# A four-layer graph network on one core: the drain of the attention layer re-ordered, the weight products taken in seven quarters, some normalising moved to GpSimd

## The chip, the core and the metric

The kernel runs on one core of a Trainium2 chip. The metric is the device time of one execution in microseconds (us); lower is better. Three runs of the kernel before took 2685.5 to 2687.25, with a median of 2686.97 us.

## The reference

Four graph layers work on x (4096 rows of 256) and one dense adjacency matrix adj (4096 x 4096), all in float32. Each layer is added to its input and normalised:

```python
x = _layernorm(x + L0(x, adj, adj, Wqkv, bqkv, Wout, bout, graph_bias))
x = _layernorm(x + L1(x, adj, W, a))
x = _layernorm(x + L2(x, adj, W, b))
x = _layernorm(x + L3(x, adj, W))
```

L0 is attention with 4 heads of 64: the scores are `qh @ kh.T / 8 + graph_bias * adj`, masked where adj is 0, then softmax, the product with v, and Wout. L1 is a graph attention: `softmax(leaky_relu(e_src[:, None] + e_dst[None, :]))` under the mask, times `x @ W`. L2 is `adj_norm @ x @ W.T + b` and L3 is `relu(adj_norm @ x @ W)`, where adj_norm is adj scaled by the inverse roots of its row sums on both sides.

## The kernel before

It is written so that the order of the instructions on each engine follows from a loop over steps (`manual_schedule`); every engine works through its own list in order and waits by semaphores.

**Layer 0 (lines 217 to 770).** A unit is 128 rows and one pair of heads; there are 64 units of four steps, and a step covers 1024 of the 4096 columns. `step(t)` (L543) runs units in a pipeline: `score` (TensorE products into two PSUM tiles `sc[0]` and `sc[1]`, L411, then VectorE adds the bias and takes the maximum, L422), four steps later `expo` (ScalarE, L438), then `turn` (sixteen transposes of 64 x 128 blocks on TensorE into one PSUM tile `ptr`, L452, and a copy to SBUF as `pt`, L460 on ScalarE or L458 on VectorE), one step later `attend` (TensorE, 32 records into `po`, L470). The row sums of a unit go from VectorE (L482 to L491) through a DMA to memory (`norm`, L493) and a second DMA that spreads them (`rb`, L514), both from GpSimd's queue; `scale` (L521) multiplies `po` with them two steps after they are sent, `finish` (L376, `pp`) applies Wout. When no unit is left to score, the last unit is drained: these are the steps nd to nd+7 (nd is 256).

Beside the last two units and the drain, the list `tail` runs the start of layer 1: the finished rows are read back in eight parts of 512 rows (`load_part`, SP's queue), the inverse deviations of all but two row blocks come from a Newton iteration (`ln_newton`, L135 to L146, its sixteen later operations on GpSimd), `norm_part` (L149, four operations of 128 x 256 on VectorE) normalises a part and writes it out from GpSimd's queue, and `turn_half` (L663) transposes a part's two column halves with four 128 x 128 transposes each into `sc[0]` or `sc[1]`, from which ScalarE (L667) or VectorE (L669) copies them. The part buffers belong to a pool of seven, which the bias tiles of layer 0 and the masks of layer 1 share. `project_ed` (L682, `ped`) and `project_w` (L163) are the first products of layer 1; the list of step nd+7 begins them.

**Layer 1 (lines 840 to 1050).** A unit is 128 rows with 4 steps. `gat_step(t)` issues for step t, in this order: `score` of t (VectorE, mask L877 and L879), `attend` of t-10 (TensorE, L938), `turn` of t-6 (VectorE, L928), `expo` of t-5 (ScalarE, L921), and `leaky` of t-2 (ScalarE, L892). The maxima of a unit are combined in its fourth to fifth step (L899 to L918), in front of the turns. `attend` of a unit needs all four of its turned blocks. The products `project_w` of the other parts fill TensorE meanwhile; DMAs of their results (`e_src`, `es_q`) run beside them.

**Layers 2 and 3 (lines 1050 to the end).** The product with adj is done by blocks of 1024 output rows (two halves of 512): 16 steps to a block, 4 blocks to a layer, and in each step 7 products of 128 x 128 by 128 x 512 (L1113) in place of 8 (a Strassen scheme), each in a PSUM bank of its own (`m0` to `m6`). VectorE forms the sums of adj blocks that they need one step ahead (`sums`, L1077 to L1080); for layer 3 a row pair is prepared at the end of a step (`prepare`, L149, L819, L822 to L826). After a block's last step `keep` copies the seven results out, `combine` forms the transposed hidden rows `hT` on VectorE in the next two steps, and `rows(n)` then multiplies 128 of them with W2 or W3: two products of 128 x 256 into the one PSUM bank that is left (`py`, L1144), and VectorE adds the result onto the row (L1161; in layer 3 after a ReLU on ScalarE, L1166 and L1167) and takes its statistics. There are eight `rows` to a block, two in each of four steps: one after the third product of the step ("mid") and one behind its last ("end"). The very last block has a routine of its own (`end`), which is not changed.

A matrix product in float32 stands in the trace as two records with a weight load each; a transpose stands as one.

Of the kernel before, what the change touches and what calls it, by code (L numbers as in the profile page):

```python
# [8 lines left out]
F32 = mybir.dt.float32  # L9
# [38 lines left out]
def tile_gnn(  # L48
# [70 lines left out]
    def ln_stats(pool, row, ci):  # L119
        st = pool.tile([P, 6], F32, tag="bnst", name="bnst")  # L120
        nc.vector.bn_stats(st, row)
        nc.vector.bn_aggr(mv[:, ci, :], st)
# [24 lines left out]

    def ln_apply(dst, src, ci):
        nc.vector.tensor_scalar(  # L149
            dst, src, mv[:, ci, 0:1], rstd[:, ci : ci + 1], ALU.subtract, ALU.mult  # L150
        )
# [43 lines left out]
    with ExitStack() as l0:  # L195
# [195 lines left out]
        class Pair:  # L391
# [53 lines left out]

            def turn(self, k, j, by_dve=False):
                pa = ps_t.tile([P, 2, CS, HD], F32, tag="tr", name="ptr")
                z = self.z[j][k]
                for c in range(CS):
                    for r in range(2):  # L450
                        half = slice(r * HD, (r + 1) * HD)
                        nc.tensor.transpose(  # L452
                            pa[:, r, c, :], z[half, c * P : (c + 1) * P], ident[half, half]
                        )
                pt = pp_.tile([P, CS, P], F32, tag="pt", name="pt")
                to = pt.rearrange("p c (r i) -> p r c i", r=2)
                if by_dve:
                    nc.vector.tensor_copy(to, pa)  # L458
                else:
                    nc.scalar.copy(to, pa)  # L460
                self.pt[j][k] = pt
# [69 lines left out]
        def step(t):  # L531
# [29 lines left out]
            if turns:  # L561
                pairs[ut].turn(kt, 0)
            if expos:
                pairs[ue].expo(ke, 1)
# [28 lines left out]
            elif edges:  # L593
                edges.pop().make_edges()
            if turns:
                pairs[ut].turn(kt, 1, by_dve=not live)
            if attends and ka == NS - 2:
# [47 lines left out]

        def norm_part(j, a0, a1):
            xs = parts[j]
            for a in range(a0, a1):
                ci = a * NJ + j
                ln_apply(xs[:, a, :], rows[ci].xr if ci == NCH - 1 else xs[:, a, :], ci)  # L650
            if a1 == NA:
                nc.gpsimd.dma_start(
                    x0.rearrange("(a j p) e -> p a j e", p=P, j=NJ)[:, :, j, :], xs
                )

        def turn_half(j, cc, by_act):

            if cc == 0:
                turned_x[j] = zp.tile([P, 2, NSB, NA, QB], F32, tag="z", name="xt1")
            xs = parts.pop(j) if cc else parts[j]  # L660
            px = sc[cc][:, 0:512].rearrange("p (a i) -> p a i", i=P)
            for a in range(NA):
                nc.tensor.transpose(px[:, a, :], xs[:, a, cc * P : (cc + 1) * P], ident)  # L663
            to = turned_x[j][:, cc, :, :, :]
            px = px.rearrange("p a (b r) -> p b a r", r=QB)
            if by_act:
                nc.scalar.copy(to, px)  # L667
            else:
                nc.vector.tensor_copy(to, px)  # L669

        def turn_part(j, split=False):
            for cc in range(2):
                turn_half(j, cc, split and cc == 0)

# [20 lines left out]
        def last_rstd():  # L695
# [10 lines left out]
        edp = []  # L706
        n0, nd = n_steps - 2 * NS, n_steps
        tail = {
            n0: [(load_weights,), (load_part, 0)],
            n0 + 1: [(load_part, 1), (weight, 0, 1)],  # L710
            n0 + 2: [(load_part, 2), (weight, 1, 1), (ln_newton, 0, NCH - 2)],
            n0 + 3: [(norm_part, 0, 0, NA)],
            n0 + 4: [(load_part, 3), (norm_part, 1, 0, NA)],
            n0 + 5: [(load_part, 4), (norm_part, 2, 0, NA)],
            n0 + 6: [(load_part, 5), (weight, 0, 0), (weight, 1, 0)],
            n0 + 7: [(norm_part, 3, 0, NA), (turn_part, 0, True)],
            nd: [(load_part, 6), (turn_part, 1), (norm_part, 4, 0, NA), (load_part, 7)],
            nd + 1: [(turn_part, 2), (norm_part, 5, 0, NA)],
            nd + 2: [(turn_part, 3), (norm_part, 6, 0, NA - 1)],
            nd + 3: [(turn_part, 4), (norm_part, 7, 0, NA - 1)],  # L720
            nd + 4: [(turn_half, 5, 0, True)],
            nd + 6: [(turn_half, 5, 1, False)],
            nd + 7: [
# [3 lines left out]
                (norm_part, 7, NA - 1, NA),  # L727
                (turn_part, 6, True),
                (turn_part, 7, True),
                (project_w, 0, 0, sc[0]),  # L730
# [116 lines left out]
    with ExitStack() as l1:  # L847
# [110 lines left out]
        def at(t):  # L958
            u, s = divmod(t, NSB)
            return (units[u], s) if 0 <= t < n_t else (None, s)  # L960

        def gat_step(t):
# [5 lines left out]
            if folds:  # L968
                folds.gather_max()
            u, s = at(t)  # L970
            if u:
# [4 lines left out]
            if u:  # L976
                u.attend(s)
            u, s = at(t - NSB - 2)
            if u:
                u.turn(s)  # L980
            u, s = at(t - NSB - 1)
# [72 lines left out]
    with ExitStack() as l2:  # L1054
# [29 lines left out]
        order = (2, 3, 0, 1, 4, 5, 6)  # L1084

        class Block:
            def __init__(self, layer, jb):
# [63 lines left out]

            def rows(self, n):

                h, s = divmod(n, NSJ)
                ci = h * NP + self.jb * NSJ + s
                py = ps_m.tile([P, 512], F32, tag="y", name="py")
                for f in range(2):
                    self.weigh(n, py, f)
                row = xc[:, ci, :]
                if self.layer == 0:  # L1160
                    nc.vector.scalar_tensor_tensor(  # L1161
                        row, py[:, 0:D], d2[:, ci : ci + 1], row, ALU.mult, ALU.add
                    )
                else:
                    r = wk.tile([P, D], F32, tag="relu", name="relu")
                    nc.scalar.activation(r, py[:, 0:D], AF.Relu, scale=d3[:, ci : ci + 1])  # L1166
                    nc.vector.tensor_tensor(row, row, r, ALU.add)  # L1167
                ln_stats(wk, row, ci)

# [122 lines left out]
        def at_step(t, when, f, *args):  # L1292
            later.setdefault((t, when), []).append((f, args))
# [6 lines left out]
        with tc.manual_schedule():  # L1300
            sums(0)
            ln_rstd(NCH - 1, NCH)
            blk = None
            for t in range(n_all):
# [20 lines left out]
                if c == NP - 1:  # L1325
# [3 lines left out]

                    r0 = t + 2 + 2 * (tl == T1 - 1)  # L1330
                    for n in range(2 * NSJ):
                        at_step(r0 + n // 2, ("mid", "end")[n % 2], blk.rows, n)
                    at_step(r0 + NSJ, "mid", block_rstd, jb)
# [6 lines left out]
                    if layer == 1:  # L1340
                        for h in range(2):
                            at_step(t + 3 + NSJ + h, "end", blk.store, h)

# [50 lines left out]
```

## Time and profile before

| | us |
|---|---|
| median of three runs | 2686.97 |
| the profiled execution | 2685.98 |
| its span from the first to the last instruction | 2684.2 |
| TensorE busy in it | 2669.1 |
| VectorE busy | 2187.9 |
| ScalarE busy | 1639.5 |
| GpSimd busy | 399.2 |

In the span layer 0 lasts until about 1366 us, its drain begins at about 1339, layer 1's row products run from 1404.9 to 1849.9 and layers 2 and 3 from 1850.1 on. A line of a timeline gives the start in us, the time it lasts, the engine (PE is TensorE, PEld its weight loads, DVE VectorE, ACT ScalarE, POOL GpSimd), the line of the kernel, the tiles written and read, the shape and the number of instructions merged in it; in brackets is the time for which the engine stood before it and what ended that. A matmul's end is modelled, so the pace of products is read from their starts.

### The profile page before, as it was taken

The page shows a single profiled execution, that of the slowest core. Times are in us where ns is not written, and L with a number is a line of the kernel's source. Part 1 is how long each engine was busy: PE and PEld are TensorE (multiplying, and loading weights), DVE is VectorE, ACT ScalarE, POOL GpSimd, SP SyncE. Part 2 cuts the span into 40 slices and gives each one's busy share as a digit, 9 for nine tenths or more (in the row PEclk, how much of TensorE's full clock was granted, in tenths as well). Part 3 has the DMA queues.
Part 4 walks back from the last instruction along what each step waited for, and adds up shares of the span by engine and source line. Part 5 has one row for each costly group of instructions (what it writes and reads, how often), then busy time and mean ns, then how long its engine had stood idle before and what let it go on. Part 6 is the DMA issues. An engine that isn't in the chain of part 4 may idle for free.

```text
span 2684.2 us, 59105 instructions
## 1 busy us (share of the span) xinstructions
PE 2669.1 (99%) x23834; PEld 1832.7 (68%) x23834; DVE 2187.9 (82%) x4120; ACT 1639.5 (61%) x2678; POOL 399.2 (15%) x701
## 2 busy tenths in 40 slices
PE   9999999999999999999999999999999999999998
PEld 6777777777777777777778888886444444444444
DVE  5999999999999999999879988886966578676565
ACT  2999999999999999999867766672100001000001
POOL 1222232232222222222220000001200000000000
PEclk9999999999999999999999999999999999999999
DMA  7444444444444444444372222222544545455543
GB/s 165 90 93 94 93 92 95 93 91 96 92 90 98 91 93 97 89 94 97 107 222 80 78 72 79 73 78 76 177 157 162 171 157 173 157 165 180 173 162 112
DMA packets 680339, 312.38 MB, mean 116 GB/s; under 512 B 554144, under 2 KB 584736, under 8 KB 680064
## 3 DMA queue, kind: packets, MB, share of 16 engines
q1 hardware_dynamic: 655968, 264.97, 39.3%
q0 software_dynamic: 22144, 42.05, 4.3%
q8 instruction: 186, 3.05, 0.5%
q10 hardware_dynamic: 1952, 1.58, 0.2%
q14 instruction: 89, 0.73, 0.1%
HBM read 262.40 MB, written 46.09 MB: 115 GB/s over the span
## 4 chain that ended last, share of the span: by engine, by line
PE 97%; DVE 1%; DMA 1%; issue 0%; POOL 0%; ACT 0%; DVEq 0%; POOLq 0%; ACTq 0%
PE m L1113 29%; PE po L470 18%; PE sc L411 17%; PE po L938 17%; PE ptr L452 11%; PE py L1144 2%; PE pv L266 1%; PE pk L245 1%; PE pp L376 1%; PE pq L354 1%; PE sc L163 0%; DVE pt L458 0%; DMA e_src<-esd 0%; DMA norm<-lt 0%; DVE z L422 0%
## 5 line engine op out<-in xcount | busy, mean ns | idle before, releaser
L422 DVE CUSTOM_DVE_ANT_0 z<-sc,bias 128x1024 f32<-128x1024 f32 x512 | 606.2, 1222 | 44.7 <-PE sc L411 44.6
L438 ACT ACTIVATE z<-z,nm 128x1024 f32<-128x1024 f32 x512 | 591.5, 1155 | 0.0
L460 ACT COPY pt<-ptr 128x1024 f32<-128x1024 f32 x507 | 511.0, 1008 | 66.6 <-PE ptr L452 66.0
L411 PE MATMUL sc<-store,qT 64*128 64x512 f32 x2048 | 504.1, 604 | 0.7 <-DVE mx L422 0.5
L470 PE MATMUL po<-pt,xc 128*64 128x128 f32 x8192 | 504.1, 276 | 0.1
L470 PEld LDWEIGHTS po<-pt,xc 128*64 128x64 f32 x8192 | 442.1, 137 | 17.7 <-DVE pt L458 0.3
L938 PE MATMUL po<-store,pt 128*128 128x257 f32 x2048 | 445.4, 379 | 1.5 <-issue 1.5
L452 PEld LDWEIGHTS ptr<-ident,z 64*128 64x128 f32 x8192 | 323.1, 138 | 177.6 <-issue 87.8
L938 PEld LDWEIGHTS po<-store,pt 128*128 128x128 f32 x2048 | 387.3, 189 | 59.5 <-issue 1.8
L452 PE MATMUL ptr<-ident,z 64*128 64x64 f32 x8192 | 357.4, 225 | 1.6 <-DVE pt L458 1.3
L1113 PE MATMUL m<-asum,ysum 128*128 128x512 f32 x672 | 324.7, 592 | 0.0
L411 PEld LDWEIGHTS sc<-store,qT 64*128 64x128 f32 x2048 | 194.4, 188 | 117.0 <-issue 108.8
L1113 PEld LDWEIGHTS m<-asum,ysum 128*128 128x128 f32 x672 | 127.7, 190 | 160.3 <-issue 139.7
L335 POOL DMA_DIRECT2D edge<-mk x256 | 143.7, 561 | 554.8 <-ACT mk L329 538.9
L1077 DVE TENSOR_TENSOR asum<-a,a 128x512 f32<-128x512 f32 x128 | 88.1, 688 | 150.8 <-PE m L1113 150.8
L1113 PE MATMUL m<-asum,store 128*128 128x512 f32 x448 | 210.5, 592 | 0.0
L1113 PE MATMUL m<-a,ysum 128*128 128x512 f32 x448 | 210.5, 592 | 0.0
L318 DVE SCALAR_TENSOR_TENSOR bias<-rt,gb,u 128x512 f32<-128x512 f32 x256 | 194.2, 759 | 9.1
L928 DVE STREAM_TRANSPOSE pt<-z 128x1024 f32<-128x1024 f32 x128 | 158.1, 1237 | 40.4 <-PE po L938 39.5
L1119 ACT COPY e<-m 128x512 f32<-128x512 f32 x28 | 16.2, 586 | 277.3 <-PE m L1113 277.3
L312 DVE STREAM_TRANSPOSE rt<-raw 128x512 f32<-128x512 f32 x256 | 180.0, 703 | 6.8 <-DMA raw<-in_adjT 6.5
L329 ACT ACTIVATE mk<-rt 128x512 bf16<-128x512 f32 x256 | 158.7, 620 | 10.0 <-DMA edge<-mk 5.9
(167 smaller groups left out, 2666.4 us busy)
## 6 DMA issues: line engine op xcount, KB each, us to landing
a<-in_adjT SPq DMA_DIRECT2D x256, 512.0 KB, 4.8
raw<-in_adjT SPq DMA_DIRECT2D x512, 128.0 KB, 3.9
edge<-mk POOLq DMA_DIRECT2D x256, 128.0 KB, 2.4
mk<-edge SPq DMA_DIRECT2D x256, 128.0 KB, 2.9
xq<-in_xT SPq DMA_DIRECT2D x32, 128.0 KB, 3.8
xr<-in_x SPq DMA_DIRECT2D x32, 128.0 KB, 3.0
x<-xs POOLq DMA_DIRECT2D x8, 512.0 KB, 6.0
xc<-x SPq DMA_DIRECT2D x8, 512.0 KB, 6.2
```

The source lines that it names most:

```text
L312: nc.vector.transpose(rt.rearrange("p (b r) -> p b r", r=QB), self.raw_now[:, half * nb : (half + 1) * nb, :],)
L318: nc.vector.scalar_tensor_tensor(self.bias[k][:, m0 : m0 + HT], rt, gb, u, ALU.mult, ALU.add)
L329: nc.scalar.activation(mk, rt, AF.Copy, accum_out=self.rs[:, j : j + 1])
L411: nc.tensor.matmul(ps[j][:, q * 512 : (q + 1) * 512], self.rows.qT[j * HD : (j + 1) * HD, self.pr, :], kT[j * HD : (j + 1) * HD, self.pr, ...
L422: nc.vector.tensor_tensor_reduce(z, sc[j], self.rows.bias[k], 1.0, NEG, ALU.add, ALU.max, self.mx[:, j, k : k + 1],)
L438: nc.scalar.activation(z, z, AF.Exp, bias=self.nm[:, j : j + 1], accum_out=self.ls[:, j, k : k + 1],)
L452: nc.tensor.transpose(pa[:, r, c, :], z[half, c * P : (c + 1) * P], ident[half, half])
L460: nc.scalar.copy(to, pa)
L470: nc.tensor.matmul(self.po[j * HD : (j + 1) * HD, 0:P], v_sb[:, ci, h * HD : (h + 1) * HD], self.pt[j][k][:, c, :], start=(ci == 0), stop= ...
L928: nc.vector.transpose(self.pt[:, :, s, :], self.z[s].rearrange("p (b r) -> p b r", r=QB))
L938: nc.tensor.matmul(self.po[:, 0 : D + 1], self.pt[:, b, :, :].rearrange("p s i -> p (s i)"), wh[:, b, :], start=(b == 0), stop=(b == NBK - 1),
L1113: nc.tensor.matmul(self.m[i], left, right, start=(c == 0), stop=(c == NP - 1))
```

## The change

There are four parts.

1. *Normalising.* `ln_newton` is issued two steps earlier (n0 in place of n0+2, where n0 is 248, the first step of the last unit but one to be scored). `norm_part` for parts 0 to 2 and three quarters of parts 6 and 7 goes to GpSimd; parts 3 to 5 stay on VectorE, one step later each.
2. *Drain.* With no scores left, the second `turn` of a step is done into `sc[1]` and directly behind the first, and before `attend`. The parts are turned into `sc[0]` alone, one half before `attend` and one behind it, by sixteen transposes of 64 rows in place of eight of 128; part j is turned in step nd+j (before: parts 0 to 4 in the steps nd-1 to nd+3, part 5 in nd+4 and nd+6). Part 7 is turned into two other PSUM tiles.
3. *Layer 1's start.* In its first ten steps `turn` is issued in front of `score` on VectorE.
4. *Weights.* The product of the hidden rows with W2 or W3 is done for both row halves at once with seven products of 128 x 128 by 128 x 128 in place of four of 128 x 128 by 128 x 256 (the Strassen scheme again). Sums of the weights are formed once and sums of `hT` once a block, on GpSimd. `weigh_shared` (four products, "mid") is copied out by ScalarE and summed up by four GpSimd operations; one step later `rows` (three products, "end") is added to that by VectorE, and both row blocks follow. The rows come two to three steps later than before, and with them the row rates, the preparation for layer 3 of the last block, and the stores.

In the program as it is built the weight sums stand in GpSimd's list in front of the first preparation of layer 2. VectorE's first operation on a layer-1 mask stands in the fourth step of the drain, between the copies of the two halves of part 3.

```diff
     def turn(self, k, j, in_scores=False):
+                if in_scores:
+                    pa = sc[1].rearrange("p (r c i) -> p r c i", r=2, i=HD)
+                else:
+                    pa = ps_t.tile([P, 2, CS, HD], F32, tag="tr", name="ptr")
...
             if turns:
                 pairs[ut].turn(kt, 0)
+            if turns and not live:
+                pairs[ut].turn(kt, 1, in_scores=True)
+            for f, *args in inner.get(t, ()):
+                f(*args)
             if expos:
                 pairs[ue].expo(ke, 1)
...
-            if turns:
-                pairs[ut].turn(kt, 1, by_dve=not live)
+            if turns and live:
+                pairs[ut].turn(kt, 1)
...
             for a in range(NA):
-                nc.tensor.transpose(px[:, a, :], xs[:, a, cc * P : (cc + 1) * P], ident)
+                for r in range(2):
+                    half = slice(r * HD, (r + 1) * HD)
+                    nc.tensor.transpose(
+                        px[:, r, a * HD : (a + 1) * HD],
+                        xs[half, a, cc * P : (cc + 1) * P],
+                        ident[half, half],
+                    )
...
+        inner = {nd + i: [(turn_half, i, 0, sc[0])] for i in range(6)}
         tail = {
-            n0: [(load_weights,), (load_part, 0)],
+            n0: [(load_weights,), (load_part, 0), (ln_newton, 0, NCH - 2)],
...
-            n0 + 2: [(load_part, 2), (weight, 1, 1), (ln_newton, 0, NCH - 2)],
-            n0 + 3: [(norm_part, 0, 0, NA)],
-            n0 + 4: [(load_part, 3), (norm_part, 1, 0, NA)],
-            n0 + 5: [(load_part, 4), (norm_part, 2, 0, NA)],
+            n0 + 2: [(load_part, 2), (weight, 1, 1)],
+            n0 + 3: [(norm_part, 0, 0, NA, gp)],
+            n0 + 4: [(load_part, 3), (norm_part, 1, 0, NA, gp)],
+            n0 + 5: [(load_part, 4), (norm_part, 2, 0, NA, gp)],
...
-            n0 + 7: [(norm_part, 3, 0, NA), (turn_part, 0, True)],
-            nd: [(load_part, 6), (turn_part, 1), (norm_part, 4, 0, NA), (load_part, 7)],
+            nd: [(turn_half, 0, 1, sc[0]), (load_part, 6), (norm_part, 3, 0, NA), (load_part, 7)],
+            nd + 1: [(turn_half, 1, 1, sc[0]), (norm_part, 4, 0, NA)],
...
-                (turn_part, 6, True),
-                (turn_part, 7, True),
+                (turn_half, 6, 0, sc[0], True),
+                (turn_half, 6, 1, sc[1]),
+                (turn_last, 7),
...
+            turns = at(t - NSB - 2)
+            soon = t < NSB + 6
+            if soon and turns[0]:
+                turns[0].turn(turns[1])
             u, s = at(t)
             if u:
                 u.score(s)
...
+            def hidden_sums(self):
+                self.hs = self.e[:, 0:4, :]
+                tt, hs, hT = nc.gpsimd.tensor_tensor, self.hs, self.hT
+                tt(hs[:, 0, :], hT[:, 1, 0, :], hT[:, 1, 1, :], ALU.add)
...
+            def weigh_shared(self, s):
+                py = ps_m.tile([P, 512], F32, tag="y", name="py")
...
+                self.small(py, 0, self.hT[:, 0, 0, rs], w[:, 0, 0:P])
+                self.small(py, 1, self.hs[:, 0, rs], ws[:, 0, :])
+                self.small(py, 2, self.hs[:, 2, rs], ws[:, 2, :])
+                self.small(py, 3, self.hs[:, 1, rs], ws[:, 1, :])
...
+                nc.scalar.copy(e[:, 0:4, :].rearrange("p i e -> p (i e)"), py)
+                tt = nc.gpsimd.tensor_tensor
+                tt(e[:, 4, :], e[:, 0, :], e[:, 3, :], ALU.add)
+                tt(e[:, 3, :], e[:, 1, :], e[:, 2, :], ALU.add)
+                tt(e[:, 3, :], e[:, 3, :], e[:, 4, :], ALU.add)
+                tt(
+                    e[:, 1:3, :],
+                    e[:, 1:3, :],
+                    e[:, 4, :].unsqueeze(1).to_broadcast([P, 2, P]),
+                    ALU.add,
+                )
...
-                for f in range(2):
-                    self.weigh(n, py, f)
...
+                self.small(py, 0, self.hT[:, 0, 1, rs], w[:, 1, 0:P])
+                self.small(py, 1, self.hs[:, 3, rs], w[:, 1, P : 2 * P])
+                self.small(py, 2, self.hT[:, 1, 1, rs], ws[:, 3, :])
+                e = self.part.pop(s)
+                c = e[:, 0:3, :].rearrange("p i e -> p (i e)")
+                nc.vector.tensor_tensor(c, c, py[:, 0 : 3 * P], ALU.add)
...
-                    r0 = t + 2 + 2 * (tl == T1 - 1)
-                    for n in range(2 * NSJ):
-                        at_step(r0 + n // 2, ("mid", "end")[n % 2], blk.rows, n)
+                    r0 = t + 2 + (tl == T1 - 1)
+                    at_step(r0, "mid", blk.hidden_sums)
+                    r0 += 2
+                    for s in range(NSJ):
+                        at_step(r0 + s, "mid", blk.weigh_shared, s)
+                        at_step(r0 + s + 1, "end", blk.rows, s)
+                    r0 += 1
```

## The prediction

> **What bounds the kernel now.** I read the page first: busy shares and the chain.
>
> ```profile
> PE 2669.1 (99%) x23834; PEld 1832.7 (68%) x23834; DVE 2187.9 (82%) x4120; ACT 1639.5 (61%) x2678; POOL 399.2 (15%) x701
> PE 97%; DVE 1%; DMA 1%; issue 0%; POOL 0%; ACT 0%; DVEq 0%; POOLq 0%; ACTq 0%
> ```
>
> TensorE is the bound nearly everywhere, so a gain is TensorE work removed or one of its few holes closed. The holes came from TensorE's timeline, 1285 to 1425 us. First, the score products of the last attention unit:
>
> ```profile
> 1317.34 1.94 PE L411 MATMUL sc<-store,qT 64*128 64x512 f32 x8
> ...
> 1322.84 2.69 PE L411 MATMUL sc<-store,qT 64*128 64x512 f32 x7 [0.53 <-DVE mx L422]
> ...
> 1328.83 1.94 PE L411 MATMUL sc<-store,qT 64*128 64x512 f32 x8
> ```
>
> Steps start 4.80 us apart before and after (1312.54 to 1317.34, 1328.83 to 1333.64); here they take 5.50 and 5.99, together 1.9 too long. VectorE's timeline names the cause: it stands 3.08 us in front of the first norm_part, and the scores queue behind it.
>
> ```profile
> 1320.27 1.38 DVE L149 TENSOR_SCALAR xs<-xs,mv,rstd 128x256 f32<-128x256 f32 x4 [3.08 <-POOL rstd L146]
> ```
>
> Second, the drain, in the chain of waits from 1325 on:
>
> ```profile
> 1345.91 1.90 PE po L470 x32
> 1347.81 0.66 PE ptr L452 x16
> ...
> 1348.50 1.24 DVE pt L458
> ...
> 1349.78 0.71 PE ptr L452 x16
> 1350.49 1.90 PE po L470 x32
> ```
>
> Both turnings of a step share one PSUM tile, so the next turning waits for VectorE's copy: 4.58 us a step. Third, the joint to layer 1 (TensorE's timeline again):
>
> ```profile
> 1371.36 1.09 PE L663 MATMUL sc<-ident,xs 128*128 128x128 f32 x8 [0.39 <-ACT xt L667]
> 1372.75 2.00 PE L163 MATMUL sc<-w_sb,xt 128*128 128x257 f32 x8 [0.29 <-ACT xt L667]
> ...
> 1404.90 20.45 PE L938 MATMUL po<-store,pt 128*128 128x257 f32 x93 [1.46 <-issue]
> ```
>
> Last, the products with W2 and W3, in TensorE's and the weight loads' timelines:
>
> ```profile
> 2665.18 1.88 PE L1113 MATMUL m<-asum,store 128*128 128x512 f32 x4
> 2666.90 1.89 PE L1144 MATMUL py<-w_sb,hT 128*128 128x256 f32 x8
> 2668.63 0.59 PE L1113 MATMUL m<-asum,ysum 128*128 128x512 f32 x1
> ```
> ```profile
> 1379.06 1.07 PEld L181 LDWEIGHTS pe<-esd,pick 128*128 128x128 f32 x8
> 1380.05 0.19 PEld L163 LDWEIGHTS sc<-w_sb,xt 128*128 128x128 f32 x1
> ```
>
> A product is two records, passes below. By the starts, a pass of 512 columns costs 1.72/4 = 0.430 us, one of 256 costs 1.73/8 = 0.216: 0.836 ns a column, so 0.109 for 128. The eight loads stand before passes of 4 columns; less the first, which waits for a 0.216 pass, they follow each other every (0.99-0.216)/7 = 0.111 us: loading is the floor, not the 0.189 of one load.
>
> **The change, part by part.** *Norms to GpSimd.* The Newton steps start two steps earlier, parts 0 to 2 are normalised on GpSimd; VectorE loses that wait and 12 operations of 0.41. A GpSimd operation of 256 elements is 0.74 (row L370) and of 30 is 0.25 (L144): 12 at up to 0.85 make 10 us, beside GpSimd's idle time. In its queue the row-sum DMA of the unit stands behind part 0 only. Gain 1.9, at least 1.0 if another VectorE wait is next.
>
> *Drain.* From the last live turning (1338.83) to the pp products (1366.18) it is 27.35 us. After, the second turning takes the free score tile, and a part's eight whole transposes (0.87) become sixteen half ones at the ptr cadence (0.65). TensorE then needs 3 x 0.65 + 1.90 = 3.85 a step. But the second half of a part stands behind the attend products, and VectorE's norm_part and next pt copy behind that: 0.33 + 0.7 + 1.3 + 1.2 + 0.6 + sync 0.15 = 4.3 in the three steps with that order. The first turning of the drain still waits for the one ptr tile (1.15), since part 0 no longer fills it. Sum: 0.65 + 1.15 + 3.85 + 3 x 4.3 + 4.4 (last sums, 0.5 late) + 3.3 = 26.25. The row sums start 2.1 us later (behind pt and xt copies) and are wanted about 1.7 earlier; before, they took until about 1351.5 from 1342.4, and waited for nobody. I add 0.5 for VectorE waiting on them: 26.75, gain 0.6. Bounds: 3.3 (TensorE alone throughout) and -1.5 (rb landing in 5.3 instead of 2.4 us, its tile's extremes). Buffers of parts come free up to a step later: SP's queue holds the last part's load and the masks behind them. Mask 0 then lands near 1353; its first use is in the fourth drain step, near 1357: nothing, unless a load takes 4 us longer.
>
> *Parts 6 and 7.* Part 7 goes to other PSUM tiles, and the first projection no longer waits for its copy. From the end of ped (1369.99) to project_w it was 2.76; after it is 0.65 + 0.87 of TensorE: gain 1.2 (0.7 to 1.4).
>
> *First unit's turns before scores.* TensorE stood 1.46 us for the fourth turn (VectorE 1403.56), queued behind a score of 1.23 and its mask though its exponential ended at 1401.52. In front, it ends near 1402.8, before the projections do at 1403.4. Later scores slip 1.2 to 1.6; the second unit's turns end near 1416.9 now and are needed 13.9 after the first attend, with nearly 1 us left. Gain 1.4 (0 to 1.46).
>
> *Seven quarter products.* In 7 blocks x 4 row groups, 8 passes of 0.216 (1.73) become 14 of 0.111 (1.55): 0.175 x 28 = 4.9. Bounds: 6.1 at 0.108 and 4.5 at 0.112. Around them each group adds an ACT copy (0.59, ACT nearly idle here), four GpSimd sums and a VectorE add of 384 (0.55 by size). GpSimd, by 0.18 + 2.2 ns an element: 3 x 0.46 + 0.74 = 2.1 a group, 4 x 1.3 = 5.2 a block. Layer 1's adding step on VectorE, the fullest: block sums 2.94 (starts 2202.59 to 2205.53), add 0.55, wait for ReLU 0.65, two rows 2.1: 6.2, beside TensorE's 14 x 0.430 + 1.55 = 7.56. VectorE's add, now one per group at the step's end, frees the single py bank 2.6 us before the next products want it. Two steps also hold a preparation (2.3): some 3 us late then, inside the step by which block sums run ahead. Cost nothing while this cover holds; up to 1 us a block if it is gone.
>
> [...] The trace:
>
> ```profile
> 1936.86 1.59 POOL L821 TENSOR_TENSOR xc<-xc,b_b 128x256 f32<-128x256 f32 x2 [4.37 <-ACT store L819]
> ```
> ```profile
> 1937.21 0.65 DVE L822 TENSOR_TENSOR ysum<-store 128x256 f32<-128x256 f32 x1 [0.66 <-ACT store L819]
> 1937.79 0.95 DVE L825 TENSOR_TENSOR ysum<-store 128x256 f32<-128x256 f32 x1
> ```
>
> Undisturbed, both take 0.43 and 0.42 (2200.97, 2201.32): 1.59 us of GpSimd cost VectorE 0.75, a share of 0.47. By the row the adding step is 6.2 + 1.0 = 7.2, under 7.56: nothing. [...] I take the row.
>
> **Sum.** 1.9 + 0.6 + 1.2 + 1.4 + 4.9 = 10.0. The profiled execution took 2685.98 (span 2684.2 and 1.8 around it), so 2676.0; the median 2686.97, 1.0 longer, gives 2677.0.
>
> **Rivals.** [...] Chance 0.15. (2) Slower: weight loads set the pace of the small products, and each pass costs a load's 0.189. Then 28 x 14 x 0.078 = 30.6 more, 2707.6. For it: every 128x128 load lasts 0.190 and no two-pass product of 128 columns runs at full clock in this trace except a pair; against: the L181 cadence. It eats the product gain from 0.124 a pass and makes the kernel slower from 0.150. Chance 0.06. (3) The change doesn't do what it says: the drain stays tied to VectorE and the row sums (-1.5) and the first attend finds another wait (0): 2677.0 + 2.1 + 1.4 = 2680.5. Chance 0.12.
>
> **Numbers.** The forecast has 0.61; 0.06 is left for what I don't see. Best ends of all parts: 1.9 + 3.3 + 1.4 + 1.5 + 6.1 = 14.2, 2672.8; worst without rival 2: 1.0 - 1.5 + 0.7 + 0 + 3 = 3.2, 2683.8. Range 2672.5 to 2684. A measurement tells about 0.2% from no change, 5.4 us: faster (below 2681.6) 0.76, same 0.15, slower (above 2692.3) 0.09.
>
> **What would show it.** Right: score products 4.8 us apart throughout; no 3 us VectorE wait on rstd; project_w some 3.7 us earlier; no hole before the first L938; py passes starting every 0.11 us with no hole around them; VectorE's adds right after py. Wrong: py passes over 0.124; holes before py or the asum products in the adding steps; a VectorE wait on rb in the third drain step; a new hole at the second layer-1 unit.

## The result, and the profile after

The changed kernel takes 2680.51 us (median of 11 runs, 2679.21 to 2683.92), the kernel before 2686.70 beside it (11 runs): ratio 0.9977, 95% interval 0.9969 to 0.9985. That is 6.2 us less, with an interval from 4.0 to 8.3. The profiled execution took 2680.28 with a span of 2678.5 (before: 2685.98 and 2684.2). Busy times and the chain, from the page of the changed kernel:

```profile
PE 2660.0 (99%) x24058; PEld 1831.2 (68%) x24058; DVE 2231.4 (83%) x4131; ACT 1653.2 (62%) x2705; POOL 544.6 (20%) x867
PE 97%; DVE 1%; DMA 1%; issue 0%; ACT 0%; POOL 0%; SPq 0%; DVEq 0%; POOLq 0%; ACTq 0%
```

TensorE is still the bound; its busy time fell by 9.1 us. The stages follow, each in TensorE's timeline. The last live scores, the drain and the joint:

```profile
1317.81 1.94 PE L411 MATMUL sc<-store,qT 64*128 64x512 f32 x8
1322.62 1.94 PE L411 MATMUL sc<-store,qT 64*128 64x512 f32 x8
...
1332.23 1.94 PE L411 MATMUL sc<-store,qT 64*128 64x512 f32 x8
```
```profile
1355.73 0.46 PE L673 MATMUL sc<-ident,xs 64*128 64x64 f32 x8 [0.66 <-DVE xt L683]
1356.03 0.66 PE L456 MATMUL ptr<-ident,z 64*128 64x64 f32 x16
1356.53 0.66 PE L456 MATMUL sc<-ident,z 64*128 64x64 f32 x16
1357.03 0.42 PE L673 MATMUL sc<-ident,xs 64*128 64x64 f32 x8
1357.38 1.97 PE L474 MATMUL po<-pt,xc 128*64 128x128 f32 x32
...
1364.13 1.08 PE L376 MATMUL pp<-wout_sb,oT 128*64 128x256 f32 x8
```
```profile
1369.47 1.91 PE L163 MATMUL sc<-w_sb,xt 128*128 128x257 f32 x8
...
1394.29 2.00 PE L163 MATMUL sc<-w_sb,xt 128*128 128x257 f32 x8 [1.61 <-ACT store L171]
...
1401.34 19.85 PE L967 MATMUL po<-store,pt 128*128 128x257 f32 x90
```

The scores are 4.80 us apart throughout. The two turnings now follow each other, and the idle 0.66 us moved in front of a part's second half. The projections start without a hole, and the first attend product (L967) has none in front of it. But inside the projections stands a hole of 1.61 us that was 0.16 before. ScalarE's timeline names its cause: the activation L921 waits for the second unit's source scores, and the copies L171, which free the projections' PSUM, queue behind it.

```profile
1392.61 1.15 ACT L921 ACTIVATE z<-z,es_q 128x1024 f32<-128x1024 f32 x1 [2.20 <-DMA es_q<-e_src]
1393.67 0.57 ACT L171 COPY store<-sc 128x514 f32<-128x514 f32 x1
```

In layers 2 and 3 the eight passes of one group (from 2279.97 to the next product at 2280.86) come every 0.111 us, with nothing idle around them:

```profile
2279.97 0.38 PE L1216 MATMUL py<-w_sb,hT 128*128 128x128 f32 x2
2280.19 0.83 PE L1216 MATMUL py<-w_sb,e 128*128 128x128 f32 x6
2280.86 1.88 PE L1166 MATMUL m<-asum,store 128*128 128x512 f32 x4
```

In the whole stage there is one new hole, in layer 3's first block, 2.36 us in all. By the starts 1.98 of it stand in front of the product at 2272.72 (its row has 1.82, counted from the modelled end of the product before), the rest in front of the next two. TensorE's row comes first, then VectorE's and GpSimd's in the same microseconds:

```profile
2272.72 1.13 PE L1166 MATMUL m<-asum,ysum 128*128 128x512 f32 x2 [1.82 <-DVE asum L1110]
```
```profile
2266.23 1.68 DVE L149 TENSOR_SCALAR xc<-xc,mv,rstd 128x256 f32<-128x256 f32 x2
2268.49 0.90 DVE L851 TENSOR_TENSOR ysum<-store 128x256 f32<-128x256 f32 x1 [0.58 <-ACT store L848]
2269.31 1.48 DVE L854 TENSOR_TENSOR ysum<-store 128x256 f32<-128x256 f32 x1
2270.72 1.35 DVE L855 TENSOR_TENSOR ysum<-store 128x128 f32<-128x128 f32 x1
2271.99 0.68 DVE L1110 TENSOR_TENSOR asum<-a,a 128x512 f32<-128x512 f32 x1
```
```profile
2266.48 1.28 POOL L1209 TENSOR_TENSOR e<-hT 128x512 f32<-128x512 f32 x1 [70.20 <-DVE hT L1191]
2267.84 1.27 POOL L1210 TENSOR_TENSOR e<-e,hT 128x512 f32<-128x512 f32 x1
2269.06 1.45 POOL L1211 TENSOR_TENSOR e<-hT 128x512 f32<-128x512 f32 x1
2270.47 1.44 POOL L1212 TENSOR_TENSOR e<-hT,e 128x512 f32<-128x512 f32 x1
```

VectorE prepares pair 11 while GpSimd makes the hidden sums of layer 2's last block. The five VectorE operations there take 5.41 us. In the kernel before, the same operations stand in the same order at this place, with nothing on GpSimd beside them:

```profile
2271.32 0.73 DVE L149 TENSOR_SCALAR xc<-xc,mv,rstd 128x256 f32<-128x256 f32 x2
2272.71 0.42 DVE L822 TENSOR_TENSOR ysum<-store 128x256 f32<-128x256 f32 x1 [0.66 <-ACT store L819]
2273.05 0.42 DVE L825 TENSOR_TENSOR ysum<-store 128x256 f32<-128x256 f32 x1
2273.39 0.28 DVE L826 TENSOR_TENSOR ysum<-store 128x128 f32<-128x128 f32 x1
2273.59 0.69 DVE L1077 TENSOR_TENSOR asum<-a,a 128x512 f32<-128x512 f32 x1
```
```profile
2276.20 1.02 PE L1113 MATMUL m<-asum,ysum 128*128 128x512 f32 x2
```

The five operations from L149 to L826 take 1.85 us. So 5.4 us of GpSimd cost VectorE 3.6, a share of 0.65. Before, the block sum ended at 2274.28, 1.9 us ahead of the product that reads it: that was VectorE's reserve here. Now the preparation also starts 0.4 us nearer to that product; 3.6 and 0.4 less 1.9 make the hole of some 2 us, in which TensorE waits for the block sum (L1110).

### The profile page after: what moved, and what is told of

The parts are those of the page before. It is cut to its first block, busy times and chain, and to the rows that moved or that the text cites. A ratio compares the mean times of both kernels' runs of the same rounds, so it can differ in the third digit from the quotient of the medians.

```text
span 2678.5 us, 59798 instructions
## 1 busy us (share of the span) xinstructions
PE 2660.0 (99%) x24058; PEld 1831.2 (68%) x24058; DVE 2231.4 (83%) x4131; ACT 1653.2 (62%) x2705; POOL 544.6 (20%) x867
## 4 chain that ended last, share of the span: by engine, by line
PE 97%; DVE 1%; DMA 1%; issue 0%; ACT 0%; POOL 0%; SPq 0%; DVEq 0%; POOLq 0%; ACTq 0%
PE m L1166 28%; PE po L474 18%; PE sc L411 17%; PE po L967 17%; PE ptr L456 11%; PE py L1216 2%; PE pk L245 1%; PE pp L376 1%; PE pq L354 1%; PE pv L266 1%; PE sc L163 0%; DMA e_src<-esd 0%; DMA es_q<-e_src 0%; DMA raw<-in_adjT 0%; PE pw L236 0%
## 5 line engine op out<-in xcount | busy, mean ns | idle before, releaser
L967 PE MATMUL po<-store,pt 128*128 128x257 f32 x2048 | 445.4, 379 | 0.0
L967 PEld LDWEIGHTS po<-store,pt 128*128 128x128 f32 x2048 | 387.3, 189 | 57.9 <-issue 0.3
L1110 DVE TENSOR_TENSOR asum<-a,a 128x512 f32<-128x512 f32 x128 | 93.4, 730 | 105.5 <-PE m L1166 105.4
L1229 ACT COPY e<-py 128x512 f32<-128x512 f32 x28 | 16.4, 587 | 250.1 <-PE py L1216 172.9
```

The costliest lines, as they stand in the source:

```text
L967: nc.tensor.matmul(self.po[:, 0 : D + 1], self.pt[:, b, :, :].rearrange("p s i -> p (s i)"), wh[:, b, :], start=(b == 0), stop=(b == NBK - 1),
```

## The experiments

The theory after these two traces: four of the five steps held; the missing 3.5 us (2680.5 against 2677.0) are the 2.4 at the joint of layers 2 and 3, where GpSimd holds VectorE, and the hole inside the projections, which is the luck of a transfer. The rivals: the turns in front of the scores gain nothing and only move the wait; the joint's hole is a full VectorE, not GpSimd.

All kernels compute everything. The ratio is to runs of the kernel before on the same chip, with its 95% interval; the median of these was 2687.22 us beside e1 to e4, 2686.72 beside e5 to e8 and 2687.14 beside e9 to e11, so half a microsecond between the medians of two lines says nothing. The next columns are read from TensorE's starts in each trace (us): idle inside the projections, first projection to first attend product, and first to last of the big products of layers 2 and 3.

| kernel | median us | ratio | hole | joint | layers 2, 3 |
|---|---|---|---|---|---|
| before | 2686.70 | | 0.16 | 32.15 | 819.79 |
| changed | 2680.51 | 0.9977 (0.9969-0.9985) | 1.61 | 31.87 | 817.57 |
| e1 products only | 2685.58 | 0.9992 (0.9983-1.0) | 2.66 | 34.63 | 817.60 |
| e2 turns behind | 2682.16 | 0.9982 (0.9973-0.9991) | 1.68 | 33.54 | 817.61 |
| e3 preparation later | 2677.53 | 0.9964 (0.9951-0.9976) | 1.66 | 31.93 | 815.21 |
| e4 rows later | 2683.36 | 0.9987 (0.9978-0.9996) | 3.04 | 34.98 | 819.30 |
| e5 turns alone | 2685.43 | 0.9995 (0.9986-1.0003) | 2.59 | 32.94 | 819.78 |
| e6 rows last | 2680.26 | 0.9976 (0.9967-0.9985) | 0.89 | 31.15 | 817.58 |
| e7 norms on VectorE | 2680.20 | 0.9975 (0.9967-0.9984) | 2.67 | 34.61 | 817.59 |
| e8 half by ScalarE | 2678.81 | 0.9971 (0.9960-0.9983) | 0.69 | 30.95 | 817.92 |
| e9 leaky later | 2678.92 | 0.9968 (0.9955-0.9980) | none | 29.99 | 817.61 |
| e10 more sums | 2684.52 | 0.9991 (0.9983-1.0) | 0.95 | 31.20 | 821.32 |
| e11 best | 2673.88 | 0.9950 (0.9936-0.9963) | none | 30.00 | 815.41 |

### e1: the seven quarter products alone

The kernel before, with the changed kernel's last stage (from the block products on) in place of its own; no line of the stages ahead is touched.

> The kernel before with only the seven quarter products (and their sums) of the change. Theory: the products are worth 0.65 us in each of 7 blocks (4.6), and the one hole of 2.4 us in front of the first block of layer 3 comes with them, since it is made by their sums on GpSimd; so the span should be 2.2 us shorter than before, with one row of an asum wait of 1.8 us near 2277 and small products at 0.112 us a pass. Rival: the hole comes from the other parts of the change, which start layers 2 and 3 earlier against the transfers; then it is absent here and the gain is 4.6.

Layers 2 and 3 take 817.60 us, 2.19 less than before, and the hole at the joint is there (again 1.98 us by the starts), with the same lengthened VectorE operations in front of it (1.68, 0.90, 1.49 and 1.35):

```profile
2279.27 1.12 PE L1133 MATMUL m<-asum,ysum 128*128 128x512 f32 x2 [1.84 <-DVE asum L1077]
```

So that hole belongs to this part and not to an earlier start. The run shows something else: its projections are those of before, line for line, and yet they hold 2.66 us of idle time where the trace of before had 0.16.

```profile
1399.26 2.00 PE L163 MATMUL sc<-w_sb,xt 128*128 128x257 f32 x8 [2.66 <-ACT store L171]
```

The same code gives 0.16 or 2.66: this hole can't be read from one trace, and the trace that the prediction was made from had a lucky landing.

### e2 and e5: the turns in front of the scores, undone and alone

```diff
-            soon = t < NSB + 6
+            soon = False
```

> The changed kernel with the first unit's turns put back behind the score of their step. Theory: the turns in front are worth their 1.4 us even in the changed kernel, and the late landing of es_q took as much away again before them; here the hole of 1.6 us inside the projections stays, a second one of about 1.4 us comes back before the first attend product, and the kernel is 1.4 us slower than the changed one (the first attend product 3.9 us or more after the end of the projections' last copy order, near 1402.7 instead of 1401.34). Rival: the turns in front made the hole inside the projections themselves, by moving VectorE's work; then that hole is gone here, one of 1.4 us stands before the first attend product, and the time is that of the changed kernel within 0.3 us.

In TensorE's timeline of e2 both holes stand one after the other:

```profile
1393.99 2.00 PE L163 MATMUL sc<-w_sb,xt 128*128 128x257 f32 x8 [1.68 <-ACT store L171]
1402.65 22.63 PE L967 MATMUL po<-store,pt 128*128 128x257 f32 x103 [1.45 <-issue]
```

The joint is 33.54 - 31.87 = 1.67 us longer than in the changed kernel, and the median 1.65 higher. e5 is the kernel before with this part alone:

```diff
+            turns = at(t - NSB - 2)
+            soon = t < NSB + 6
+            if soon and turns[0]:
+                turns[0].turn(turns[1])
             u, s = at(t)
             if u:
                 u.score(s)
...
-            u, s = at(t - NSB - 2)
-            if u:
-                u.turn(s)
+            if not soon and turns[0]:
+                turns[0].turn(turns[1])
```

> The kernel before with only the first unit's turned blocks in front of the scores. Theory: this part is worth its 1.4 us, and the hole inside the projections is a thing of the transfer that brings the source scores, with or without the change (0.16 in the trace of before, 2.66 in the same code of the run with the products alone). So the hole before the first attend product (1.46 us) is gone here, whatever the one inside the projections is, and the kernel is 1.4 us faster than before; that inner hole lies anywhere from 0.1 to 2.7. Rival: it only moves the wait, so the kernel is within 0.4 us of before and a hole before the first attend product remains.

```profile
1399.50 2.00 PE L163 MATMUL sc<-w_sb,xt 128*128 128x257 f32 x8 [2.59 <-ACT store L171]
1406.56 33.63 PE L938 MATMUL po<-store,pt 128*128 128x257 f32 x154
```

No idle time stands before L938 any more, and the other hole is 2.59, in the range that the text named. Without that hole the joint is 30.35 us (32.94 - 2.59); that of e1, which has the turns behind, is 31.97 (34.63 - 2.66). The median gained 1.3 (2686.72 to 2685.43), though the interval reaches no change. Both runs agree with a gain of 1.4 to 1.7. A hole of 1.45 or 1.46 us stands before the first attend product in the three traces with the turns behind (before, e1, e2) and in none of the ten with the turns in front, whatever the other hole is: the rival "only moved" falls.

### e3: pairs 10 and 11 prepared three steps later

```diff
-                            free = (NJB - 1) * NP + p + NSJ + 2
+                            free = (NJB - 1) * NP + p + NSJ + 2 + 3 * (p in (10, 11))
```

> The changed kernel with the preparation of pairs 10 and 11 for layer 3 three steps later, so that no VectorE preparation lies beside GpSimd's sums of hidden rows of layer 2's last block. Theory: the hole of 2.4 us before layer 3's first steps was VectorE held by GpSimd during that preparation; it goes, no new one comes, and the kernel is 2.4 us faster than the changed one. Rival: VectorE is simply full there (seven copies, nine combining operations, block sums of 2.9), or the sums would hold up the combining as much; then at least 1.5 us of the hole stays or returns two or three steps later.

Layers 2 and 3 take 815.21 us, 2.36 less than the changed kernel, the size of the hole, and there is no other. GpSimd's hidden sums still hold VectorE, but now its block sums (e3, VectorE and GpSimd):

```profile
2264.02 2.28 DVE L1111 TENSOR_TENSOR asum<-a,a 128x1024 f32<-128x1024 f32 x1
2266.23 1.75 DVE L1112 TENSOR_TENSOR asum<-a 128x512 f32<-128x512 f32 x1
2267.90 1.75 DVE L1113 TENSOR_TENSOR asum<-a 128x512 f32<-128x512 f32 x1
2269.57 1.75 DVE L1110 TENSOR_TENSOR asum<-a,a 128x512 f32<-128x512 f32 x1
```
```profile
2265.30 2.13 POOL L1210 TENSOR_TENSOR e<-e,hT 128x512 f32<-128x512 f32 x1
2267.39 1.71 POOL L1211 TENSOR_TENSOR e<-hT 128x512 f32<-128x512 f32 x1
2269.06 1.71 POOL L1212 TENSOR_TENSOR e<-hT,e 128x512 f32<-128x512 f32 x1
```

Each VectorE operation takes 1.06 us longer than alone (1.22 and 0.69), whatever its own length, and both engines' operations start 1.67 us apart (2267.90 to 2269.57, 2267.39 to 2269.06): here they took turns, one operation each. VectorE loses 4.2 us here, more than the 3.6 in the changed kernel, and TensorE loses nothing. The same holds in the changed kernel's six other blocks: beside the four hidden sums VectorE loses 4.1 to 4.3 us in each, and no hole follows. What decides is not the hold but the reserve: behind the combining and two preparations VectorE had only 1.9 us of it. Moving VectorE's work alone could not tell a held VectorE from a full one; the kernel before, with the same work and no hole, and e10 do.

### e10: the hold dosed

Two further sums of 512 on GpSimd behind each block's four, thrown away:

```diff
                 tt(hs[:, 3, :], hT[:, 0, 1, :], hs[:, 1, :], ALU.subtract)
+                for i in range(2):
+                    tt(self.e[:, 4, :], hT[:, i, 0, :], hs[:, i, :], ALU.add)
```

> The changed kernel with two further sums of 512 on GpSimd behind the four hidden sums of every block, their results thrown away. GpSimd works 3.3 us longer a block there. Theory: GpSimd takes 0.6 to 0.7 of its time from VectorE's operations on two inputs, 2.0 to 2.3 us more; at the joint of layers 2 and 3, where VectorE has nothing left, the hole grows from 2.4 to 4.4 to 4.7 us; in the other blocks the reserve holds it and no hole comes; the kernel is 2.0 to 2.4 us slower than the changed one. Rival: the joint's hole is not dosed by GpSimd's work (it stays at 2.4 within 0.5), or the other blocks have no reserve either, then each loses up to 2 us, 10 and more in all.

No other block gets a hole. The joint's grows, but by 3.75 us (821.32 - 817.57) where 2.0 to 2.4 was expected. 2.1 of it is VectorE held by the two further sums: L1110 and L1111 took 1.75 and 2.28, 1.06 longer each. The other 1.7 is something that the expectation did not have: TensorE's clock. Two rows of the table by stretches of e10 show it (the columns are the stretch, its length, busy time and count of PE, PEld, DVE, ACT and POOL, then the granted clock, the DMA share and GB/s):

```profile
2275.00:2277.00 2.00, 1.65 (x2) 0.84 (x3) 2.00 (x4) 0.00 (x0) 0.00 (x0) 0.54 0.00 0
2277.00:2279.00 2.00, 2.00 (x4) 0.86 (x3) 2.00 (x4) 0.00 (x0) 0.00 (x0) 0.61 0.76 225
```

After the hole the passes come every 0.85 us instead of 0.43 until 2278.8.

### e4 and e6: the reload of the rows moved

```diff
-        filling[5].append((load_rows,))
+        filling.setdefault(9, []).append((load_rows,))
```

> The changed kernel with the reload of the rows (4 MB) issued four layer-1 steps later, behind the masks of the third unit. Theory: the hole of 1.6 us in the projections stands because the small transfer of the source scores is queued in the DMA engines behind this reload, which didn't start earlier when TensorE did; here it lands in under 5 us instead of 7.3, the hole is gone and the first attend product starts 1.4 to 1.6 us earlier, the kernel is that much faster. Rival: the landing depends on the small transfer's own fixed cost or on the masks; then it stays at 6 to 7 us and the hole at 1 us or more; or the rows come too late for the first unit's end (a new wait of VectorE there).

The theory fell. The first hop (to DRAM) was shorter, GpSimd's wait for it 4.82 us instead of 6.78, but ScalarE's wait for the second was 3.62 instead of 2.20, and the hole 3.04. The parts of the reload landed from 1378.2 to 1390.5, so it lay beside the shorter first hop (1379.6 to 1384.7) as well as beside most of the second. Two halvings of the clock, 1.7 us each, came with it in this trace, one of them in layer 3 (819.30 against 817.57). e6 has step 13 for 9:

> The changed kernel with the reload of the rows issued eight layer-1 steps later, behind the masks of the fourth unit and the loads of the last weights. Issued four steps later, the reload lay over the second hop of the source scores and the hole grew from 1.6 to 3.0 us. Theory: the hole is bulk traffic in the same DMA engines as the two small hops; here both hops run beside masks alone, each takes under 5 us, the hole of 1.6 is gone, the first attend product starts 1.4 to 1.6 us earlier. Rival: masks alone hold the hops as long (then the hole stays above 1 us), or the reload now lies over the third and fourth transfers or lands after the first unit's end, and a new wait of over 1 us stands in the attend products after 1405.

The first hop takes 4.48, the hole is 0.89, the joint 0.7 us shorter. But GpSimd's wait for the third transfer is 6.77 instead of 4.67, a hole of 0.56 appears in the second unit, and the median is that of the changed kernel: no gain. The reload landed from 1387.3 to 1400.2 here, over the whole first hop of the second transfer too, which waited 5.18 (3.76 to 5.67 in the eleven traces with the reload in its place). So these two runs, one trace each, do not show that bulk traffic holds the small hops.

### e9: the waiting instruction moved

```diff
-            u, s = at(t - 2)
+            u, s = at(t - 4)
             if u:
                 u.leaky(s)
```

> The changed kernel with the activation that uses the source scores (ScalarE, leaky) two layer-1 steps later for every unit, so that in ScalarE's queue the second unit's first one stands behind the first unit's last exponential. Theory: the hole inside the projections (0.2 to 3.0 us in eight traces) is ScalarE standing in its order for the second unit's source scores, with the projections' copies queued behind it; two steps later the transfer has landed whatever its luck, the hole is gone, from the first projection to the first attend product it is 30.0 to 30.4 us instead of 31.9, and the kernel is 1.5 to 2 us faster than the changed one. Rival: the copies find another wait (the first unit's last exponential, or VectorE's turn), and the first attend product starts within 0.5 us of where it does now.

Measured: 29.99 us from the first projection to the first attend product, no hole, and no wait for the transfer in ScalarE's timeline, though GpSimd's wait for the first hop was as long as ever (6.22).

```profile
1391.09 3.64 PE L163 MATMUL sc<-w_sb,xt 128*128 128x257 f32 x16
1394.57 1.90 PE L163 MATMUL pm<-w_sb,xt 128*128 128x257 f32 x8
1396.30 3.64 PE L163 MATMUL sc<-w_sb,xt 128*128 128x257 f32 x16
1399.78 2.55 PE L967 MATMUL po<-store,pt 128*128 128x257 f32 x11
```

The median is 1.6 us lower, and the five executions lie within 0.57 us of each other (the changed kernel's eleven within 4.7). Of the transfer's luck nothing is left, so the cause of this hole is shown: ScalarE's order behind a transfer whose landing varies.

### e7: parts 0 to 2 normalised on VectorE

```diff
-            n0 + 3: [(norm_part, 0, 0, NA, gp)],
-            n0 + 4: [(load_part, 3), (norm_part, 1, 0, NA, gp)],
-            n0 + 5: [(load_part, 4), (norm_part, 2, 0, NA, gp)],
+            n0 + 3: [(norm_part, 0, 0, NA)],
+            n0 + 4: [(load_part, 3), (norm_part, 1, 0, NA)],
+            n0 + 5: [(load_part, 4), (norm_part, 2, 0, NA)],
```

> The changed kernel with parts 0 to 2 normalised on VectorE again, the Newton steps still two steps earlier. Theory: of the 1.9 us in the last live unit, VectorE's wait of 3.08 us for the Newton result was the larger cause; with it gone, 12 operations of 0.41 on VectorE cost at most 0.5 us, because its step has that room. Rival: VectorE's step of 4.8 us is full, so each norm part of 1.3 us pushes the scores behind it, the two or three steps take 5.3 us or more, and at least 1.2 us of the gain goes.

The score steps stay 4.80 apart (1313.15, 1317.96, 1322.77, 1327.57, 1332.37) with three norm parts between them on VectorE, and the median is the same. So with the earlier Newton steps in place, moving the operations to GpSimd adds nothing to the 1.9 us. Its hole in the projections was 2.67, and the clock halved behind it:

```profile
1395.00:1397.00 2.00, 1.39 (x4) 1.12 (x5) 0.17 (x1) 2.00 (x5) 1.96 (x4) 0.69 1.07 227
1397.00:1399.00 2.00, 2.00 (x6) 1.63 (x5) 1.73 (x3) 1.60 (x3) 0.82 (x3) 0.50 1.06 213
```

### e8: the drain's first halves copied by ScalarE

```diff
-        inner = {nd + i: [(turn_half, i, 0, sc[0])] for i in range(6)}
+        inner = {nd + i: [(turn_half, i, 0, sc[0], True)] for i in range(6)}
```

> The changed kernel with the first half of each part in the drain copied by ScalarE instead of VectorE. Theory: in the drain the second half waits 0.6 to 0.8 us a step for VectorE's chain of turn copy, half copy and norm part, as the prediction's 4.3 us a step said; without that copy the chain is 0.6 shorter, the drain from the last live turning to the last sums becomes 1.5 to 2.5 us shorter, and so does the kernel. Rival: ScalarE (two exponentials, one turn copy, one half copy, 4.1 us a step) then sets the same pace, and the gain stays under 0.7 us.

```profile
1358.96 0.46 PE L673 MATMUL sc<-ident,xs 64*128 64x64 f32 x8 [0.86 <-DVE xt L683]
1359.35 1.97 PE L474 MATMUL po<-pt,xc 128*64 128x128 f32 x32
...
1361.71 1.08 PE L376 MATMUL pp<-wout_sb,oT 128*64 128x256 f32 x8
```

From the last live score product to the last one of pp it is 29.14 us, in the changed kernel 31.25: 2.1 less, and the median 1.7. (Over the changed kernel and the seven experiments with the same drain it is 30.94 to 31.66, so this is no scatter.) Most steps no longer wait before the second half; one wait of 0.34 and one of 0.86 are left. VectorE's chain did set the drain's pace, as the prediction said.

### e11: three edits together

The edits of e3, e8 and e9.

> The changed kernel with three edits: pairs 10 and 11 prepared three steps later, the activation with the source scores two steps later, the first halves in the drain copied by ScalarE. Theory: the three lie in different stages and add up, 2.4 and 1.7 and 1.9, 6.0 us faster than the changed kernel, about 2674.5, with no hole over 0.9 us from the last live scores to the end but those at the very start of layer 2. Rival: the gain of the drain is lost again in the wait for the transfers that it doesn't move (rows, source scores), so only 4 us or less remain.

2673.88 us, 6.6 under the changed kernel; the span fell from 2678.5 to 2671.8. The gains add up: joint 30.00, layers 2 and 3 815.41, drain 28.67. It is faster than the kernel before by 0.50% (interval 0.37 to 0.64).

## Why the prediction was right in its sign and 3.5 us too good

The time (2677.0 forecast, 2680.5 measured) lies in the range, between the forecast and the slow end. Step by step:

| step | forecast | measured | from |
|---|---|---|---|
| live scores | 1.9 | 1.89 | last live score, less a start 0.48 later in the second trace |
| drain | 0.6 | 0.57 | last live score product to pp, both by their starts |
| parts 6 and 7 | 1.2 | 1.30 | pp to the first projection |
| turns before scores | 1.4 | 1.45 to 1.67 | hole in e2; joints of e5 (1.62) and e2 (1.67); 0.28 in the two first traces |
| quarter products | 4.9 | 4.57 | a block 0.65 shorter, 7 blocks |
| hold of VectorE by GpSimd | 0 | -2.36 | hole at the joint of layers 2 and 3 |

With 1.45 for the turns that makes 7.4, inside the interval of 4.0 to 8.3; the 1.2 us between it and the 6.2 of the medians are traced to no step. The spans differ by 5.7, since they also hold the later start (0.48) and the unlucky landing (1.61 against 0.16).

**The step that failed** is the end of the quarter products: "Cost nothing while this cover holds", priced by "I take the row". Two things were wrong in it, a size and a place. The size: the share of 0.47 came from a row in which GpSimd's operation overlapped two VectorE operations and idle time; where VectorE works without a pause the share is 0.60 (e3) to 0.65 (the joint). In e3 the starts are 1.67 us apart on both engines, and each VectorE operation loses 1.06 us. For the four hidden sums, 5.2 us by the prediction's own estimate, the row gives 2.4 us of VectorE; measured were 3.6 at the joint and 4.1 to 4.3 in the six other blocks. So the price was too low, but the price did not decide.

The 1 us a block that the prediction put on a lost cover is shown by no run: six of seven blocks lost nothing, nor did any adding step, and the one hole, 2.36 us, stands at the joint. In the adding steps GpSimd cost VectorE less than the row: nothing for two of a block's four groups, whose sums fall where VectorE stands idle, and mostly 0.53 us for the other two, where the row had 1.0. The cover held: in layer 3's second block an adding step of 7.5 us (2388.54 to 2396.08) has 0.87 us left on VectorE.

The place: the prediction weighed the cover in the adding steps and did not look at the four hidden sums in the step where layer 2 ends, where VectorE also combines and prepares two pairs. e1 shows the hole with this part alone, e3 closes it by moving VectorE's work, e10 makes it larger with GpSimd's.

**Turns before scores.** The step was right, its size too (e2, e5). What stood against it in the two traces is a transfer whose landing differs by more than the step is worth. The prediction gave this wait no term: the 0.16 us of idle time there passed for a property of the kernel. Over three traces with the stages of before it was 0.16, 2.66 and 2.59, over the changed kernel and the experiments that leave drain, reload and ScalarE's order alone 1.61, 1.68, 1.66, 2.67 and 0.95: means of 1.80 and 1.71, no difference that so few and so scattered traces could show. Why the same code lands so differently was not found, and e4 and e6 do not show that bulk traffic is part of it.

**Norms to GpSimd.** Right in the sum, wrong in its reading: without the wait, the 12 operations cost nothing on VectorE either (e7). The estimate of up to 0.85 us for a GpSimd operation of 256 elements was too low, too: 1.23 in the mean of 18. **Drain and parts 6 and 7** went as worked out: of the three steps with VectorE's chain, for which 4.3 us each was expected, two take 4.27 from one attend to the next, and e8 confirms that chain as the cause. A wait on `rb`, which the prediction had as a sign of being wrong and for which its sum held 0.5 us, did come in the other, which takes 4.64:

```profile
1351.77 0.29 DVE L525 TENSOR_TENSOR oT<-po,rb 128x128 f32<-128x128 f32 x1 [0.77 <-DMA rb<-norm]
```

That 0.57 meets 0.6 so closely is partly luck: in the seven other traces with this drain the gain is 0.16 to 0.88, in the mean of all eight 0.45.

**Rivals 2 and 3** are out: a small pass costs 0.111 us, not 0.189, and the drain did what was said. One sum in rival 2 is wrong: without the products the other parts gain 5.1 us, so the kernel would have become slower from 0.137 us a pass, not from 0.150.

## What to carry to other kernels

Before work goes to GpSimd, look for the one step where VectorE has no reserve, not at the average step: count there about 1 us of VectorE for each GpSimd sum of 512 beside it (3.6 to 4.3 for four in this kernel), and move either. An idle stretch behind a transfer in a single trace is a draw, not a size (0.16 to 2.67 us here); if an engine's queue holds copies behind the instruction that waits for it, the waiting instruction is what to move, not the traffic (e9 against e4 and e6). And when a wait goes together with the work that stood behind it, test which of the two paid.

## What the hardware showed

Small fp32 passes of 128 columns, each with its own weights, run at 0.111 us without further loss, though one weight load lasts 0.19: the loads overlap (in the group of eight shown with the result the first lasts from 2279.97 to 2280.16 and the second starts at 2280.08).

TensorE's granted clock fell to half for 3.4 us behind holes of 2 to 3 us, in e7, twice in e4 and in e10, and each time cost 1.7 us on top of the hole. It did not fall behind holes of 2.66 (e1) and 2.59 (e5), and of the eight traces with the joint's hole of 2.0 it fell in one (e4). Where the idle time lies seems to decide this. In the traces of the kernels before and after, the clock stays at full from its first rise to its one fall behind the last products, for 2672.64 and 2665.81 us. These are 783.0 and 781.0 times 3.413 us, and the falls inside the work of e4, e7 and e10 last 3.40 by the tables of granted clock. The rest is an estimate, worked out from the starts of the products in the traces, with windows of 3.413 us counted from the first rise and each pass taken at 0.84 ns a column. By it the four windows at whose end the clock halved (the fall behind the last products left aside) hold 2.86 and 2.28 (e4), 2.83 (e7) and 2.56 us (e10) without products; no other window from 1380 us up to the last products holds more than 2.17 (in the kernel before 1.63, in the changed one 1.98). The holes of e1 and e5 were each cut by the end of a window, with 2.10 and 2.07 us idle in the fuller one. So by this estimate the four windows followed by half the clock had a third of their time or less in products, and all others more. It is read from traces made for other questions; no run moved a hole against the windows. What was measured is that idle time of 2 to 3 us cost 1.7 us on top four times, and other holes of that size did not.
